# Local attention on patches of 8x4 instead of 8x8 pixels, in narrower tensor-engine tiles, and the two halves of a windowed sum issued together

## The chip, the cores and the metric

The kernel runs on one core of a Trainium2 chip, in one launch, in float32. The metric is device time in microseconds (us). Before the change the median of three runs is 1379.91 us (1377.02 to 1380.01).

The engines are called by the names of the profile: PE is the tensor engine (PEld its weight loads), DVE the vector engine, ACT the scalar engine, POOL the GpSimd engine, SP the engine that issues most DMAs. A "block" is eight image rows, 512 pixels, of one of four images.

## The reference

The input is x of 4 x 256 x 64 x 64. Layer 0 is an attention of each pixel over its 3x3 neighbours; layer 1 works on the 4096 tokens of an image: a gated sum over a window of 64 tokens, then a mixture of eight experts of which each token takes two.

```python
# layer 0: x = x + local attention of the group-normed x
q = (xc @ Wq + bq) * scale                      # every pixel
kf, vf = p @ Wk + bk, p @ Wv + bv               # padded image
logits = einsum('bhwc,bhwnc->bhwn', q, Kw)      # the 9 neighbours
ctx = einsum('bhwn,bhwnc->bhwc', softmax(logits), Vw)
out = ctx @ Wo + bo
...
# layer 1
g = sigmoid(tanh(x @ Wp.T + bp) @ Wg.T)
t = t + windowed_sum(g * x, 64) / windowed_sum(g, 64)   # x is the layer-normed t
t = t + sum over the top-2 experts of weight * (gelu(x @ w1[e] + b1[e]) @ w2[e] + b2[e])
```

## The kernel before, in words

There are 32 blocks (`NB`), 8 to an image. Weights are folded at the start (Wq with Wk, Wv with Wo), so that keys and values are the pixels themselves.

**Attention of a block** is in two generators. `produce(g)` projects the pixels to queries (`psq`, L509: four products of 512 columns) and writes them patch by patch. A patch is 8x8 pixels, its keys are the 10x10 pixels around, 100 in all (`NKEY`). A bias row is made by `psr` (L527, eight products whose outputs are 32 partitions high, so they lie in four column tiles of PE), taken up by ACT (`qrow`, L532) and turned by `psb` (L536). The logits `pss` (L547) are, for each of four groups of 128 pixels (`NG`), two patches by two channel halves: 16 products of 64 output rows and 100 columns. DVE adds the mask that keeps the 3x3 neighbours and takes the maximum (L554), ACT makes the exponentials (`pe`, L563) and their sums. `attend(g)` turns the weights with four transposes (`ptp`, L610), copies them on ACT (`pT`, L612), and mixes the pixels of the patch (`psc`, L621): 8 products over 100 keys, 64 output rows, 256 columns. ACT divides (`mix`, L627). Then come four-by-two transposes (`ptm`, L636), the output product (`pso`, L648) and the residual. The pixels by patch, `xp`, come from DRAM in a layout made beforehand (patch keys on partitions), loaded two blocks ahead (`load_xp`); `edges` overwrites the image's rim with the mean, on SP.

**Layer 1 of a block.** `tail(g)` transposes to tokens (`ptx`, L672), projects (`psp`, L685), makes the gate (`pj`, `z`: tanh and exp on ACT), copies the rows for the window (`wl`, L726 to L728) and sums over 64 tokens by two band matrices, `bandl` for the lower 64 outputs and `band` for the upper 64 (L736 and L737; 64 output rows each, so two column tiles). It does so three times a block: `psg` (36 columns) and `psw` twice (512 columns). Then it normalises, chooses the experts and makes the rows to be sent. `ranks(g)` counts (`psk`) and sends each token's row to its two experts' queues in DRAM with indirect DMAs on POOL (L870, eight a block).

**Experts.** `experts()` takes 135 slots of 256 rows: it fetches the rows (`sx`, SP), transposes them (`ptx`, L1023), copies on ACT (L1027), multiplies by w1 (`psh`, L1035), takes the gelu on ACT (`h`, L1041), multiplies by w2 (`psy`, L1054), adds the bias and weights on DVE (L1058, L1059), and adds the rows to the output with two indirect DMAs on POOL (L1072). A pair of these waits until the pair before has landed.

**Order.** All engines run their instructions in order. The main loop steps the generators `attend(g)`, `ranks(g-2)`, `tail(g-1)` and `produce(g+1)` in turn, and after each step lets the experts' stream go on as far as a table of due slots says (`follow`, 27 steps a block). The Tile framework then orders each engine's instructions by priority (place in this emission) and by its own estimate of when operands are ready. PSUM tiles come from `ps_a` (five buffers, all of the attention and tail) and `ps_s` (three, the experts).

```python
def window(to, part):
    nc.tensor.matmul(to[0:WIN], bandl, wl[part], start=True, stop=True)
    nc.tensor.matmul(to[WIN:P], band[:, WIN:P], wx[part], start=True, stop=True)
```

Of the kernel before, what the change touches and what calls it, by code (L numbers as in the profile page):

```python
# [46 lines left out]
FP = mybir.dt.float32  # L47
AF = mybir.ActivationFunctionType
# [4 lines left out]
P = 128  # L53
# [9 lines left out]
def hybrid_block_kernel(ctx: ExitStack, tc: tile.TileContext, ins: dict, out: bass.AP):  # L63
    nc = tc.nc
    x = ins["x"]
    B, C, FW, _ = x.shape
    W = FW - 2
    HW = W * W
    NC = C // P
    TB = 512  # L70
# [4 lines left out]
    WIN = 64  # L75
# [1 line left out]
    SCALE = float(C) ** -0.5  # L77
    EPS = 1e-5
    XBUFS = 4
    TH, TW = TB // W, 8  # L80
    KH, KW = TH + 2, TW + 2
    NKEY = KH * KW
    NP = W // TW
    QP = TH * TW
    NG = NP * QP // P
    PROWS = ins["xp"].shape[1]
    AHEAD = NBI + 2
    FETCH = 2
    I32, U32 = mybir.dt.int32, mybir.dt.uint32
# [20 lines left out]
    const = ctx.enter_context(tc.tile_pool(name="const", bufs=1))  # L110
    xsp = ctx.enter_context(tc.tile_pool(name="xsp", bufs=2))
    xp = ctx.enter_context(tc.tile_pool(name="xp", bufs=XBUFS))
    xtp = ctx.enter_context(tc.tile_pool(name="xtp", bufs=2))
    xpp = ctx.enter_context(tc.tile_pool(name="xpp", bufs=2))
    w1p = ctx.enter_context(tc.tile_pool(name="w1p", bufs=1))
    w2p = ctx.enter_context(tc.tile_pool(name="w2p", bufs=2))
# [5 lines left out]
    ps_a = ctx.enter_context(tc.tile_pool(name="ps_a", bufs=5, space=PSUM))  # L122
# [17 lines left out]
    def load_xp(g):  # L140
        if g >= NB:
            return
        t = xpp.tile([PROWS, NP, C], FP, tag="xp", name=f"xp_{g}")
        nc.sync.dma_start(t, ins["xp"][g])
        xpat[g] = t

# [70 lines left out]
    ident = const.tile([P, P], FP, tag="ident", name="ident")  # L217
# [26 lines left out]
    nc.vector.tensor_single_scalar(at_p[:, 1:2], at_p[:, 1:2], TW - 1, op=ALU.bitwise_and)  # L244
    nc.vector.tensor_copy(at_f, at_p)
    mask = const.tile([P, NKEY], FP, tag="mask", name="mask")
    near = w2p.tile([P, 2, KH, KW], FP, tag="pe", name="near")
    for d in range(2):
        nc.gpsimd.iota(
            near[:, d], pattern=[[1 - d, KH], [d, KW]], base=-1, channel_multiplier=0,  # L250
# [2 lines left out]
        part = near[:, d].rearrange("p a b -> p (a b)")  # L253
# [5 lines left out]
    )  # L259
    nc.vector.tensor_scalar(mask, mask, -NEG, NEG, ALU.mult, ALU.add)  # L260


    pick = const.tile([P, NG], FP, tag="pick", name="pick")
    nc.gpsimd.memset(pick, 0.0)
# [5 lines left out]
    band = const.tile([P, P], FP, tag="band", name="band")  # L270
# [9 lines left out]
    bandl = const.tile([P, WIN], FP, tag="bandl", name="bandl")  # L280
# [105 lines left out]
    for c in range(NC):  # L386
        cols = slice(c * P, (c + 1) * P)
        both = range(NC)
        ps = product(qk, [(wqT[:, o, cols], wkT[:, o, :]) for o in both], C, f"qk{c}")
# [79 lines left out]
    def edges(g):  # L469

        b, i = divmod(g, NBI)
        if g >= NB:
            return
        t, row = xpat[g], mean_row[b][0]
        rim, mean = xt[g], norm[b][0]
        nc.gpsimd.tensor_copy(
            rim[:, :, :, 0 : W + 2 : W + 1],
            mean.unsqueeze(2).unsqueeze(3).to_broadcast([P, NC, KH, 2]),
        )
        for at in ([0] if i == 0 else []) + ([KH - 1] if i == NBI - 1 else []):  # L480
            nc.gpsimd.tensor_copy(
                rim[:, :, at, :], mean.unsqueeze(2).to_broadcast([P, NC, W + 2])
            )
        lo = 1 if i == 0 else 0
        hi = KH - 1 if i == NBI - 1 else KH
        for at, h in ((0, 0), (KW - 1, NP - 1)):
            nc.sync.dma_start(
                t[lo * KW + at : (hi - 1) * KW + at + 1 : KW, h, :],
                row.partition_broadcast(hi - lo),
            )  # L490
        for kh in ([0] if lo else []) + ([KH - 1] if hi < KH else []):
            nc.sync.dma_start(
                t[kh * KW : (kh + 1) * KW],
                row.partition_broadcast(KW).unsqueeze(1).to_broadcast([KW, NP, C]),
            )

    def produce(g):
        if g >= NB:
            return
        b, i = divmod(g, NBI)  # L500
        _, rc, _ = norm[b]
        qks, qbb, ubs, kb = ask[b]
        t = xt[g]

        q = w2p.tile([P, NC, TB], FP, tag="q", name=f"q_{g}")
        for co in range(NC):
            ps = ps_a.tile([P, TB], FP, tag="a", name=f"psq_{g}_{co}")
            for ci in range(NC):
                nc.tensor.matmul(  # L509
                    ps.rearrange("p (r w) -> p r w", w=W),  # L510
                    qks[:, ci, co * P : (co + 1) * P], t[:, ci, 1 : TH + 1, 1 : W + 1],
                    start=(ci == 0), stop=(ci == NC - 1),
                )
            nc.scalar.activation(  # L514
                q[:, co].rearrange("p (h r c) -> p r h c", r=TH, c=TW),
                ps.rearrange("p (r h c) -> p r h c", r=TH, c=TW),
                AF.Identity, bias=qbb[:, co : co + 1], scale=rc[:, co : co + 1],
            )
            yield


        ps = ps_a.tile([P, P], FP, tag="a", name=f"psr_{g}")
        for ci in range(NC):
            for n in range(NG):
                to = ps[32 * n : 32 * (n + 1)].rearrange("p (j r c) -> p r j c", r=TH, c=TW)
                keys = t[:, ci, 1 : TH + 1, 1 + n * W // NG : 1 + (n + 1) * W // NG]
                nc.tensor.matmul(  # L527
                    to, ubs[:, ci, :], keys.rearrange("p r (j c) -> p r j c", c=TW),
                    start=(ci == 0), stop=(ci == NC - 1),
                )  # L530
        rows = w2p.tile([P, P], FP, tag="qrow", name=f"qrow_{g}")
        nc.scalar.activation(rows, ps, AF.Identity, bias=kb)  # L532
        yield
        qdotb = w2p.tile([P, NG], FP, tag="qdotb", name=f"qdotb_{g}")
        ps = ps_a.tile([P, NG], FP, tag="a", name=f"psb_{g}")
        nc.tensor.matmul(ps, rows, pick, start=True, stop=True)  # L536
        nc.vector.tensor_copy(qdotb, ps)
        yield

        top = w4p.tile([P, NG], FP, tag="stop", name=f"stop_{g}")  # L540
        s = w2p.tile([P, NG, NKEY], FP, tag="s", name=f"s_{g}")
        ps = ps_a.tile([P, NG, NKEY], FP, tag="a", name=f"pss_{g}")
        for n in range(NG):
            for ci in range(NC):
                for j in range(P // QP):
                    h = n * P // QP + j
                    nc.tensor.matmul(  # L547
                        ps[j * QP : (j + 1) * QP, n].rearrange("p (a b) -> p a b", b=KW),
                        q[:, ci, h * QP : (h + 1) * QP], t[:, ci, :, h * TW : h * TW + KW],
                        start=(ci == 0), stop=(ci == NC - 1),  # L550
                    )
        yield
        for n in range(NG):
            nc.vector.tensor_tensor_reduce(  # L554
                out=s[:, n], in0=ps[:, n], in1=mask, scale=1.0, scalar=NEG,
                op0=ALU.add, op1=ALU.max, accum_out=top[:, n : n + 1],
            )
        nc.vector.tensor_add(top, top, qdotb)
        nc.vector.tensor_sub(top, qdotb, top)
        pe = w2p.tile([P, NG, NKEY], FP, tag="pe", name=f"pe_{g}")  # L560
        den = w4p.tile([P, NG], FP, tag="den", name=f"den_{g}")
        for n in range(NG):
            nc.scalar.activation(  # L563
                pe[:, n], s[:, n], AF.Exp, bias=top[:, n : n + 1],
                accum_out=den[:, n : n + 1],
            )
        nc.vector.reciprocal(den, den)
        soft[g] = pe, den
        yield
# [16 lines left out]
    latest = []  # L586
# [12 lines left out]
    def attend(g):  # L599
        if g >= NB:  # L600
            return
        b, i = divmod(g, NBI)
# [2 lines left out]
        _, rc, back = norm[b]  # L605


        pt = ps_a.tile([P, NG, P], FP, tag="a", name=f"ptp_{g}")
        for n in range(NG):
            nc.tensor.transpose(pt[0:NKEY, n, :], pe[:, n, :], ident)  # L610
        pT = w2p.tile([P, NG, P], FP, tag="pT", name=f"pT_{g}")
        latest.append(nc.scalar.copy(pT[0:NKEY], pt[0:NKEY]).ins)  # L612
        yield

        mix = w1p.tile([P, NG, C], FP, tag="mix", name=f"mix_{g}")
        for pair in range(0, NG, 2):
            ps = ps_a.tile([P, 2, C], FP, tag="a", name=f"psc_{g}_{pair}")
            for n in range(2):
                for j in range(P // QP):
                    h = (pair + n) * P // QP + j  # L620
                    nc.tensor.matmul(  # L621
                        ps[j * QP : (j + 1) * QP, n, :],
                        pT[0:NKEY, pair + n, j * QP : (j + 1) * QP], xp_[0:NKEY, h, :],
                        start=True, stop=True,
                    )
            for n in range(2):
                nc.scalar.mul(mix[:, pair + n, :], ps[:, n, :], den[:, pair + n : pair + n + 1])  # L627
        load_xp(g + 2)
        edges(g + 2)
        yield  # L630
# [30 lines left out]
    def tail(g):  # L661
# [71 lines left out]
        rden = w2p.tile([P, NT], FP, tag="rden", name=f"rden_{g}")  # L733

        def window(to, part):
            nc.tensor.matmul(to[0:WIN], bandl, wl[part], start=True, stop=True)  # L736
            nc.tensor.matmul(to[WIN:P], band[:, WIN:P], wx[part], start=True, stop=True)  # L737

        ps = ps_a.tile([P, NT, 1 + E], FP, tag="a", name=f"psg_{g}")
        window(ps, (slice(None), slice(None), slice(C, C + 1 + E)))  # L740
# [478 lines left out]
```

## Time and profile before

| | |
|---|---|
| median of three runs | 1379.91 us |
| the profiled execution, its own time | 1383.41 us |
| its span | 1381.7 us |
| mean granted PE clock | 0.959 |
| PE passes (matmuls as the profile counts them) | 7148 |
| ACT table loads | 106, 1283 ns each |
| moved by DMA | 205.45 MB, 149 GB/s |
| patch loads `xp` | 32 of 896 KB |

A product in float32 shows as two passes in the profile. A busy time of PE holds a modelled tail after each pass, so the distance from one run's start to the next is the better price. In the page, a row of tenths has 40 slices of 34.5 us. In the timeline a row is a run of like instructions: start, length, engine, line, what is written from what, rows*columns of the weights, and how many passes.

### The profile page before, as it was taken

The numbers are of one execution on the slowest core, as the hardware profiler recorded it, in microseconds if no ns is written. First come the engines' busy times: TensorE is split into PE (matmuls) and PEld (weight loads), VectorE is DVE, ScalarE is ACT, GpSimd is POOL, SyncE is SP. The second block draws the span as 40 slices with busy tenths as digits, with TensorE's granted clock in tenths as the row PEclk, the third lists the DMA queues.
The fourth block names the chain that finished last, engine by engine and source line by source line (L and its number), as shares of the span: only waits on it lengthen the run. The fifth ranks groups of instructions, "written<-read, shape, count | busy, mean of one in ns | idle before, by whom it ended". The sixth has DMA issues, their size and how long they took to land. (4 is left out here: it accounts for less than half of the span.)

```text
span 1381.7 us, 24884 instructions
## 1 busy us (share of the span) xinstructions
PE 1215.3 (88%) x7148; PEld 845.7 (61%) x7148; DVE 882.3 (64%) x4298; ACT 824.5 (60%) x1619; POOL 736.7 (53%) x645
## 2 busy tenths in 40 slices
PE   5877879899999999999999999999999998957670
PEld 4543446566666766666666666666676666646560
DVE  4376767777776757676877677677756777722230
ACT  1445556677677667767677677767766675523320
POOL 2013223656565655566665656565665666754444
PEclk9998889999999999999999999999999999989995
DMA  9774555566766666676766566656676446665443
GB/s 306 190 237 136 134 161 154 153 162 151 166 165 165 172 149 166 168 166 160 164 156 149 132 171 137 150 124 163 147 156 134 100 98 140 151 144 83 85 65 38
DMA packets 138054, 205.45 MB, mean 149 GB/s; under 512 B 15697, under 2 KB 108609, under 8 KB 134209
## 3 DMA queue, kind: packets, MB, share of 16 engines
q1 hardware_dynamic: 84256, 131.48, 32.8%
q0 software_dynamic: 51168, 71.07, 28.6%
q10 hardware_dynamic: 2496, 1.32, 0.3%
q8 instruction: 59, 0.97, 0.3%
q14 instruction: 75, 0.61, 0.2%
HBM read 113.23 MB, written 90.59 MB: 148 GB/s over the span
## 5 line engine op out<-in xcount | busy, mean ns | idle before, releaser
L1072 POOL DMA_INDIRECT out<-sx x270 | 428.4, 1587 | 394.8 <-DVE sx L1059 69.6
L1054 PE MATMUL psy<-w,h 128*128 x1080 | 295.2, 397 | 31.0 <-DVE sx L1058 28.5
L870 POOL DMA_INDIRECT rows_in<-tok,rows x256 | 254.8, 995 | 105.5 <-issue 72.7
L1054 PEld LDWEIGHTS psy<-w,h 128*128 128x128 f32 x1080 | 193.8, 192 | 137.5 <-DVE sx L1058 70.8
L1035 PE MATMUL psh<-xc,w1s 128*128 128x256 f32 x1080 | 271.0, 393 | 1.3 <-ACT h L1041 1.1
L1035 PEld LDWEIGHTS psh<-xc,w1s 128*128 128x128 f32 x1080 | 201.4, 195 | 56.7 <-issue 23.1
L1058 DVE TENSOR_TENSOR sx<-psy,b2b 128x256 f32<-128x256 f32 x270 | 113.7, 421 | 161.7 <-PE psy L1054 137.1
L1041 ACT ACTIVATE h<-psh,w1s 128x256 f32<-128x256 f32 x270 | 112.9, 468 | 95.6 <-PE psh L1035 81.5
L1027 ACT COPY xc<-ptx 128x512 f32<-128x512 f32 x135 | 78.8, 584 | 139.1 <-PE ptx L1023 126.6
L648 PE MATMUL pso<-mixT,vo 128*128 128x512 f32 x256 | 127.2, 605 | 3.7 <-ACT mixT L637 1.9
L1023 PE MATMUL ptx<-ident,sx 128*128 128x128 f32 x540 | 85.9, 280 | 47.9 <-DMA sx<-rows_in 46.4
L509 PE MATMUL psq<-x,qks 128*128 128x512 f32 x256 | 126.0, 615 | 0.6 <-PE ptx L672 0.6
L1023 PEld LDWEIGHTS ptx<-ident,sx 128*128 128x128 f32 x540 | 67.3, 147 | 74.6 <-issue 48.9
L1059 DVE TENSOR_SCALAR sx<-sx 128x256 f32<-128x256 f32 x270 | 97.1, 360 | 3.7 <-DVE kb L463 0.3
L514 ACT ACTIVATE q<-psq,qbb,irc 128x512 f32<-128x512 f32 x64 | 49.7, 777 | 67.5 <-PE psq L509 62.9
L1016 ACT COPY w1s<-w1b 128x514 f32 x135 | 83.4, 619 | 6.6 <-DVE given L929 2.1
L554 DVE CUSTOM_DVE_ANT_0 s<-pss,mask 128x100 f32<-128x100 f32 x128 | 25.8, 257 | 89.0 <-PE ptx L1023 33.8
L769 ACT ACTIVATE x<-x,scale 128x256 f32<-128x256 f32 x128 | 66.4, 589 | 16.6 <-DVE scale L765 12.7
L737 PE MATMUL psw<-wx,band 128*64 128x512 f32 x128 | 74.1, 675 | 0.0
L736 PE MATMUL psw<-wl,bandl 128*64 128x512 f32 x128 | 73.7, 672 | 0.0
L685 PE MATMUL psp<-wpr,x1c 128*128 128x136 f32 x512 | 72.5, 284 | 0.0
L685 PEld LDWEIGHTS psp<-wpr,x1c 128*128 128x128 f32 x512 | 66.5, 191 | 4.9 <-ACT mix L627 2.3
(218 smaller groups left out, 2076.6 us busy)
## 6 DMA issues: line engine op xcount, KB each, us to landing
sx<-rows_in SPq DMA_DIRECT2D x135, 272.0 KB
xp<-in_xp SPq DMA_DIRECT2D x32, 896.0 KB
x<-in_x SPq DMA_DIRECT2D x32, 660.0 KB
xs<-in_xs SPq DMA_DIRECT2D x32, 512.0 KB
out<-x SPq DMA_DIRECT2D x32, 512.0 KB
out<-sx POOLq DMA_INDIRECT x270
rows_in<-tok,rows POOLq DMA_INDIRECT x256
rows_in<-blank SPq DMA_DIRECT2D x9, 272.0 KB
```

The source lines that it names most:

```text
L509: nc.tensor.matmul(ps.rearrange("p (r w) -> p r w", w=W), qks[:, ci, co * P : (co + 1) * P], t[:, ci, 1 : TH + 1, 1 : W + 1], start=(ci == ...
L648: nc.tensor.matmul(ps, vo[:, ci, co * P : (co + 1) * P], mixT[:, ci, :], start=(ci == 0), stop=(ci == NC - 1),)
L685: nc.tensor.matmul(ps[:, u, :], xc[:, ci, t * P : (t + 1) * P], wpr[:, ci, :], start=(ci == 0), stop=(ci == NC - 1),)
L870: return nc.gpsimd.indirect_dma_start(out=rows_in[:, :], out_offset=bass.IndirectOffsetOnAxis(ap=rows[:, c, t : t + 1], axis=0), in_=tok[: ...
L1016: nc.scalar.copy(w1s, w1b[:, e, :])
L1023: nc.tensor.transpose(pt[:, c, t * P : (t + 1) * P], xs[:, t, c * P : (c + 1) * P], ident)
L1035: nc.tensor.matmul(ps[:, f, :], w1s[:, o : o + P], xc[:, ci, :], start=(ci == 0), stop=(ci == NC - 1),)
L1041: inst = nc.scalar.activation(h[:, f, :], ps[:, f, :], AF.Gelu, bias=w1s[:, F1 + f : F1 + f + 1])
L1054: nc.tensor.matmul(ps[:, t, :], h[:, f, t * P : (t + 1) * P], w2[:, e, f, :], start=(f == 0), stop=(f == NC - 1),)
L1058: nc.vector.tensor_add(ys[:, t, :], ps[:, t, :], b2b[:, e, :])
L1059: nc.vector.tensor_scalar_mul(ys[:, t, :], ys[:, t, :], xs[:, t, bass.ds(e + C, 1)])
L1072: inst = nc.gpsimd.indirect_dma_start(out=out, out_offset=bass.IndirectOffsetOnAxis(ap=xs[:, t, C + E : C + E + 1].bitcast(U32), axis=0), ...
```

## The change

- Patches are 8x4 pixels: 60 keys (6x10) for 32 pixels, 16 patches a block; a group of 128 pixels holds four.
- The logits become 32 products of 32 output rows and 60 columns, in four column tiles.
- The exponentials are written into two lasting tiles whose rows are padded with zeros from 60 to 64 keys, so that two groups are turned by one 128x128 transpose: two transposes in place of four, and the copy `pT` has 256 columns on 128 partitions in place of 512 on 100.
- The weights of even groups then lie on partitions 0 to 63 and those of odd groups on 64 to 127. The pixels by patch are laid out likewise (128 partitions, 8 patches deep; 1024 KB in place of 896). The mixes become 16 products over 60 keys, 32 output rows, 256 columns, in two row halves by four column tiles; the halves write two PSUM tiles, which are open at the same time.
- The bias row's products stand directly before the logits; its ACT step, `psb` and the copy of its result come after them, and the generator has one stop less (five in place of six).
- In the windowed sum the upper half's product is given priority 0 and is ordered behind the lower half's, so that nothing goes between.
- `edges` writes a rim row in two DMAs, one for each half of the partitions.

```diff
-    TH, TW = TB // W, 8
+    TH, TW = TB // W, 4
...
+    HALF = P // 2
...
-        t = xpp.tile([PROWS, NP, C], FP, tag="xp", name=f"xp_{g}")
+        t = xpp.tile([P, NP // 2, C], FP, tag="xp", name=f"xp_{g}")
...
+    pes = []
+    for n in range(2):
+        t = const.tile([P, NG, HALF], FP, tag=f"pe_{n}", name=f"pe_{n}")
+        nc.gpsimd.memset(t, 0.0)
+        pes.append(t)
...
         for kh in ([0] if lo else []) + ([KH - 1] if hi < KH else []):
-            nc.sync.dma_start(
-                t[kh * KW : (kh + 1) * KW],
-                row.partition_broadcast(KW).unsqueeze(1).to_broadcast([KW, NP, C]),
-            )
+            for half in range(2):
+                at = half * HALF + kh * KW
+                nc.sync.dma_start(
+                    t[at : at + KW],
+                    row.partition_broadcast(KW).unsqueeze(1).to_broadcast([KW, NP // 2, C]),
+                )
...
-        ps = ps_a.tile([P, P], FP, tag="a", name=f"psr_{g}")
+        pr = ps_a.tile([P, P], FP, tag="a", name=f"psr_{g}")
...
-        rows = w2p.tile([P, P], FP, tag="qrow", name=f"qrow_{g}")
-        nc.scalar.activation(rows, ps, AF.Identity, bias=kb)
-        yield
-        qdotb = w2p.tile([P, NG], FP, tag="qdotb", name=f"qdotb_{g}")
-        ps = ps_a.tile([P, NG], FP, tag="a", name=f"psb_{g}")
-        nc.tensor.matmul(ps, rows, pick, start=True, stop=True)
-        nc.vector.tensor_copy(qdotb, ps)
-        yield
...
         yield
+        rows = w2p.tile([P, P], FP, tag="qrow", name=f"qrow_{g}")
+        nc.scalar.activation(rows, pr, AF.Identity, bias=kb)
+        qdotb = w2p.tile([P, NG], FP, tag="qdotb", name=f"qdotb_{g}")
+        pb = ps_a.tile([P, NG], FP, tag="a", name=f"psb_{g}")
+        nc.tensor.matmul(pb, rows, pick, start=True, stop=True)
+        nc.vector.tensor_copy(qdotb, pb)
+        yield
...
-        pe = w2p.tile([P, NG, NKEY], FP, tag="pe", name=f"pe_{g}")
+        pe = pes[g % 2]
...
-        pt = ps_a.tile([P, NG, P], FP, tag="a", name=f"ptp_{g}")
-        for n in range(NG):
-            nc.tensor.transpose(pt[0:NKEY, n, :], pe[:, n, :], ident)
+        pt = ps_a.tile([P, NG // 2, P], FP, tag="a", name=f"ptp_{g}")
+        for pair in range(NG // 2):
+            nc.tensor.transpose(
+                pt[:, pair, :], pe[:, 2 * pair : 2 * pair + 2, :].rearrange("p n k -> p (n k)"), ident
+            )
...
+        ps = [
+            ps_a.tile([P, NG // 2, C], FP, tag="a", name=f"psc_{g}_{half}") for half in range(2)
+        ]
+        for pair in range(NG // 2):
+            for half in range(2):
+                rows = slice(half * HALF, half * HALF + NKEY)
                 for j in range(P // QP):
                     nc.tensor.matmul(
+                        ps[half][j * QP : (j + 1) * QP, pair, :],
+                        pT[rows, pair, j * QP : (j + 1) * QP],
+                        xp_[rows, pair * P // QP + j, :],
                         start=True, stop=True,
                     )
...
         def window(to, part):
-            nc.tensor.matmul(to[0:WIN], bandl, wl[part], start=True, stop=True)
-            nc.tensor.matmul(to[WIN:P], band[:, WIN:P], wx[part], start=True, stop=True)
+            one = nc.tensor.matmul(to[0:WIN], bandl, wl[part], start=True, stop=True)
+            at = tc.cur_priority
+            tc.cur_priority = 0
+            two = nc.tensor.matmul(to[WIN:P], band[:, WIN:P], wx[part], start=True, stop=True)
+            tc.cur_priority = at
+            tc.add_manual_dep(
+                two.ins, one.ins.name,
+                mybir.DependencyInfo(
+                    mybir.DependencyClass.NoSync, mybir.DependencyReason.SCHED_ONLY
+                ),
+                reason="column tiles side by side",
+            )
```

## The prediction

> **What bounds the kernel now.** I read the page first, then busy time by stretches, then the timeline of the tensor engine over two blocks, the waits and the chain that ended last. The page's busy shares and its slices:
>
> ```profile
> PE 1215.3 (88%) x7148; PEld 845.7 (61%) x7148; DVE 882.3 (64%) x4298; ACT 824.5 (60%) x1619; POOL 736.7 (53%) x645
> ...
> PE   5877879899999999999999999999999998957670
> ```
>
> The tensor engine (PE) is nearly full from slice 7 to slice 33 of 40 and loose at both ends. The busy time by stretches (columns: core, stretch, its length, then busy time and count of each engine, granted clock, DMA share, GB/s) says how full:
>
> ```profile
> 600.00:800.00 200.00, 196.28 (x1189) 136.01 (x1188) 144.89 (x712) 141.81 (x272) 119.78 (x102) 1.00 0.67 157
> ...
> 1200.00:1250.00 50.00, 35.81 (x163) 29.44 (x162) 12.54 (x32) 15.93 (x33) 28.61 (x21) 0.86 0.66 153
> ```
>
> From 600 to 800 us PE is busy 98%, at full clock; VectorE (DVE) and ScalarE (ACT) 72% and 71%. From the logits of block 7 (225 us) to those of block 28 (986 us) it is 36.2 us a block. After 1200 us PE has slack. There the chain that ended last holds (start, length, what):
>
> ```profile
> 1267.54 3.95 DMA out<-sx
> ...
> 1272.34 1.55 POOL out L1072
> ...
> 1274.20 3.86 DMA out<-sx
> ```
>
> One pair of scatter-adds waits for the pair before it: a step of 6.5 us (issue 0.7, POOL 1.55, landing 3.9), 28 steps, 182 us to the end. No matmul lies in that path most of the time. So the block phase (to about 1200 us) is priced by PE, the last 180 us are not touched.
>
> The timeline of PE (start, length with its tail, passes as xN) gives the prices; the distance to the next start is what a run costs:
>
> ```profile
> 621.77 1.05 PE L736 MATMUL psw<-wl,bandl 128*64 128x512 f32 x2
> 622.95 1.13 PE L1054 MATMUL psy<-w,h 128*128 x4
> 624.01 1.07 PE L737 MATMUL psw<-wx,band 128*64 128x512 f32 x2
> ...
> 629.35 1.04 PE L672 MATMUL ptx<-ident,x1c 128*128 128x128 f32 x8
> 630.22 1.03 PE L1054 MATMUL psy<-w,h 128*128 x4
> ...
> 631.52 1.89 PE L509 MATMUL psq<-x,qks 128*128 128x512 f32 x4
> 633.34 1.95 PE L621 MATMUL psc<-xp,pT 100*64 100x256 f32 x16
> 635.22 1.99 PE L1035 MATMUL psh<-xc,w1s 128*128 128x256 f32 x8
> 637.05 1.09 PE L685 MATMUL psp<-wpr,x1c 128*128 128x136 f32 x8
> ...
> 644.15 0.68 PE L527 MATMUL psr<-x,ubs 128*32 128x128 f32 x16
> 644.76 1.99 PE L1035 MATMUL psh<-xc,w1s 128*128 128x256 f32 x8
> ```
>
> Each product is two passes. Eight 128-column transposes take 0.87 us (629.35 to 630.22): 0.109 us each, so 0.85 ns a column, 0.216 us for 256 columns, 0.432 for 512. **Column tiles do run side by side:** the 16 mix passes (64 columns wide, in two tiles) take 1.88 us where one after the other they would take 3.46; the 16 passes of the 32-wide psr take 0.61 where 16 x 0.109 is 1.74. **Going into a tiled run and out of it costs 0.344 us:** psq takes 1.82 for 4 x 0.432 = 1.73, psc 1.88 for 8 x 0.216 = 1.73, the psh behind it 1.83 for 1.73: 0.09 + 0.15 + 0.10. The same sum around paired psw runs is 0.344 too, every time.
>
> **The change part by part (PE).** Blocks are 32.
>
> Mixes (L621): 8 products of two tiles become 16 of eight tiles (two row halves by four columns). Now 8 rounds x 0.216 = 1.73 us; with eight at once 4 x 0.216 = 0.86. Row halves side by side are shown by no row. From both sides: 0.86 saved if they overlap fully, about -0.1 if not at all (8 rounds of four tiles, with 7 ns a round as psr has over its 0.108). [...] I take 0.80: 25.6 us over 32 blocks.
>
> Logits (L547): 16 products of 100 columns in two tiles, 16 rounds of 0.087 (the starts in the trace) = 1.39 us; after: 32 products of 60 columns in four tiles, 16 rounds of 60 x 0.85 = 0.051 plus psr's 7 ns: 0.93. Saved 0.46, 14.7 us in all. [...] The trace has the nearer row: within a psr round four starts lie 6.5 ns apart, and the 16 one-column passes of pqb L456 start within 0.13 us, 9 ns apart. [...]
>
> Transposes (L610): four of 0.109 become two: 0.22 saved, 7.0 us. ACT's copy of their result goes from 512 to 256 columns (586 to about 370 ns by the 256-column rows), the exponentials and mask steps from 100 to 60 columns: about 0.35 us of ACT and 0.16 of DVE a block, hidden today.
>
> Windows: in the order of the two programs 20 of 96 sums, 19 of them 512 columns wide, have an expert's matmuls between their halves, as at 621.77 and 624.01 above; none has after. A split one costs 4 x 0.432, a joined one 2 x 0.432: 19 x 0.864 = 16.4 us.
>
> Runs: the program of before goes into tiled runs 173 times, that of after 109 (psr stands directly before pss and has the same four tiles, the window runs merge): 64 x 0.344 = 22.0 us.
>
> PE's work falls by 25.6 + 14.7 + 7.0 + 16.4 + 22.0 = 85.7 us; some 3.4 us of the 36.2 of a steady block.
>
> **What else moves.** The patch load grows from 896 to 1024 KB (4 MB on 205, issued two blocks ahead, DMA share 0.67): nothing. Edges write the same two columns; a row of the rim is now two DMAs on SP instead of one, 8 more in all, behind the patch load and ahead of the next loads: below 0.1 us each at issue (the chain's SP pieces are 0.03), nothing. The steady zero padding is two fills at the start, when PE waits for data. The qrow step now follows pss, so its psb waits for ACT behind pso, as before. The loss is on ACT: in the order after, 14 blocks have a gelu between the first exponential and the other three, and the table loads go from 106 to 134. 28 x 1.283 us (the load's mean) = 36 us more on ACT, in a steady block of this kind 2.6 us on 25.6, less 0.35: 27.8 of some 33 us, 84%. Behind these loads on ACT stands the gelu h; psy waits for h, and everything behind psy on PE for that. ACT waits for psh today (81.5 us in all), so part is hidden: I charge a third, 12 us (ends 0 and 36).
>
> **The sum.** The 23 steady blocks hold 71 of the 85.7 us (1.48 each = 34; 16.4; 60 runs = 21). Off go 12 for the tables, and 9 for new waits: PE waits 0.9 us a block today (36.2 less 33.2 for all passes of a block at 0.85 ns a column, and six runs of 0.344) and the other engines come to 80%; I take a doubling on ten of the blocks. That leaves 50. The six blocks before experts run (27 us each with PE some 75% busy) hold 10; half counts, 5. The last three lie where scatter-adds already follow at 6.5 to 7 us (from 1144 us on): 1 of 5. Together 56: the profiled execution took 1383.4 us (span 1381.7), so 1327; the median of the runs shown, 1379.9, is 3.5 lower: 1324.
>
> **The rivals.**
> - Nothing is lost to waits: 71 + 8 = 79 us, 1301. For it: DVE and ACT end below 85%. Against: in-order engines with no slack left.
> - Row halves do not overlap: the mixes save nothing, some 22 us less: 1346. Only a trace can tell.
> - ACT takes most of it: the 36 us of table loads fall on PE in full, and the adds, at four pairs a block (26 us at 6.5, POOL's eight give instructions of 1 us between), hold it at times: 24 + 12 less, 1360.
> - Slower: the exponential, first in line on ACT, waits for DVE's maximum (the waits have ACT pe on DVE stop at up to 5.9 us), and the gelu queued behind it keeps psy, and with it all of PE, standing. In the 14 blocks with split exponentials PE loses this and two table loads. It decides from 85.7/14 = 6.1 us a block on; at 5.9 + 2.6 = 8.5 the loss is 119, 33 more than PE saves: 1413. Against it: today that wait comes four times in all, early, where PE is idle anyway.
>
> **Chances.** As summed, 1305 to 1340: 0.55. Nothing lost: 0.14. No row overlap: 0.10. ACT takes most: 0.10. Within 0.3%, about what a measurement of this kernel can tell from none: 0.04, all of these losses at once. Slower: 0.07. Range 1292 to 1366. Faster 0.89, same 0.04, slower 0.07.
>
> **What would show it.** A psc run of 32 passes in about 1.0 us against 1.9; psr and pss together about 1.6 against 2.2; no psy between psw halves; PE's busy time down by 80; blocks of 33.5 us; the last 28 add steps at 6.5 us still. Wrong it would be if psc stays at 1.9 (row halves in turn), if pss comes near 1.9 (a floor per start), or if waits of psy on ACT h appear by tens of us.

## The result and the profile after

The changed kernel takes 1389.63 us (median of 20 runs, 1382.23 to 1397.74) against 1380.34 for the kernel before (20 runs): ratio 1.006, 95% interval 1.0039 to 1.0081. It is slower by 0.6%. The profiled execution takes 1394.86 us, its span 1392.9, its mean granted clock 0.942 where it was 0.959. I had said 1324.

The page of the kernel after: busy times, then two of its rows of tenths.

```profile
PE 1169.3 (84%) x8620; PEld 833.3 (60%) x8620; DVE 878.7 (63%) x4298; ACT 844.5 (61%) x1647; POOL 739.9 (53%) x647
...
PE   5978799799988989899988999999899888867770
...
PEclk9999889999999999999999999999999999889995
```

PE is busy for 46 us less, and yet the program is longer: PE's share has gone from 88% to 84%. The row of tenths has eights and sevens where the row of before had nines from slice 7 on. By the start of `psr` in each block, the changed kernel is 22 us ahead at block 7 (198 us against 220) and 11 us behind at block 31: the loss falls in the steady blocks. The stretch from 600 to 800 us (columns as in the prediction):

```profile
600.00:800.00 200.00, 181.19 (x1357) 129.35 (x1356) 138.74 (x689) 145.72 (x271) 119.96 (x102) 0.97 0.62 152
```

PE is busy 181.2 us of 200 where it was 196.3, at 0.97 of the clock where it was 1.00. No other engine has risen to be the bound (ACT 73%, DVE 69%). So what is lost is waiting, and part of it slower clock.

**What came as priced.** Timeline of PE, kernel after, one block:

```profile
664.18 0.62 PE L748 MATMUL psw<-wl,bandl 128*64 128x512 f32 x1
664.19 0.62 PE L751 MATMUL psw<-wx,band 128*64 128x512 f32 x1
664.64 0.59 PE L748 MATMUL psw<-wl,bandl 128*64 128x512 f32 x1
...
670.30 1.09 PE L632 MATMUL psc<-xp,pT 60*32 60x256 f32 x32
671.32 1.99 PE L1057 MATMUL psh<-xc,w1s 128*128 128x256 f32 x8
...
681.95 0.68 PE L536 MATMUL psr<-x,ubs 128*32 128x128 f32 x16
682.44 1.04 PE L547 MATMUL pss<-x,q 128*32 128x60 f32 x38
683.90 0.33 PE L547 MATMUL pss<-x,q 128*32 128x60 f32 x4 [0.43 <-issue]
684.65 0.32 PE L547 MATMUL pss<-x,q 128*32 128x60 f32 x5 [0.41 <-issue]
685.43 0.47 PE L547 MATMUL pss<-x,q 128*32 128x60 f32 x17 [0.47 <-issue]
685.83 3.23 PE L1057 MATMUL psh<-xc,w1s 128*128 128x256 f32 x8
```

The mixes `psc` take 1.02 us (670.30 to 671.32) against 1.88: the eight 64x32 tiles of a round start 6 to 7 ns apart and overlap (four rounds at 0.216 are 0.86). The two halves of a window sum start 5 to 13 ns apart in all 192 pairs of passes. Both were forecast. The logits were not: from 682.44 to 685.83 `pss` takes 3.39 us. It breaks off after 38 passes, and then comes in pieces of 4 and 5 passes, about 0.77 us apart. "issue" says that it waited for nothing that the profile shows. In other blocks the same 64 passes take 0.98 us.

**The larger loss** is a wait of `psy`. Timeline of all engines, kernel after:

```profile
713.01 0.28 DVE L356 TENSOR_SCALAR ve_a<-tmv_a 128x4 f32<-128x4 f32 x1
...
713.62 0.98 POOL L892 DMA_INDIRECT rows_in<-tok,rows  x1 [0.31 <-issue]
...
714.91 0.96 POOL L892 DMA_INDIRECT rows_in<-tok,rows  x1 [0.30 <-issue]
...
716.18 0.96 POOL L892 DMA_INDIRECT rows_in<-tok,rows  x1 [0.30 <-issue]
717.16 1.06 POOL L357 TENSOR_TENSOR trstd_a<-ve_a,nhalf 128x4 f32<-128x4 f32 x1
...
718.25 0.61 DVE L703 SCALAR_TENSOR_TENSOR pj<-psp,trstd_a,bp 128x128 f32<-128x128 f32 x2 [2.62 <-POOL trstd_a L357]
718.78 0.17 DVE L706 COPY y<-psp 128x16 f32<-128x16 f32 x1
718.86 0.41 DVE L1080 TENSOR_TENSOR sx<-psy,b2b 128x256 f32<-128x256 f32 x1
...
719.33 1.13 PE L1076 MATMUL psy<-w,h 128*128 x4 [2.71 <-DVE sx L1080]
...
720.29 1.65 PE L648 MATMUL ptm<-ident,mix 128*128 128x128 f32 x8
```

Read it from the bottom. PE stands 2.71 us, since `psy` needs the PSUM tile that DVE's `sx` empties. DVE stands 2.62 us ahead of `sx`, at `pj`, which needs the root of the first norm, `trstd_a`. The root is a 1.06 us instruction on POOL (`pow`). Its input was ready at 713.3, but in POOL's order it stands behind four sends, 1.28 us each; the first began at 712.3, so three of them make the wait. The queues of three engines stand in line, PE behind DVE behind POOL, and none of the three is full. And after the pause PE runs at half clock for 3.4 us: the eight `ptm` transposes show 1.65 us where others of that shape show 1.04.

In other blocks the experts' scatter-adds (`out`) stand ahead of the root too. Timeline of POOL, kernel after:

```profile
750.56 1.64 POOL L1094 DMA_INDIRECT out<-sx  x1 [0.31 <-issue]
752.51 1.00 POOL L892 DMA_INDIRECT rows_in<-tok,rows  x1 [0.30 <-issue]
753.81 0.97 POOL L892 DMA_INDIRECT rows_in<-tok,rows  x1 [0.30 <-issue]
754.81 1.05 POOL L357 TENSOR_TENSOR trstd_a<-ve_a,nhalf 128x4 f32<-128x4 f32 x1
```

The sums by waits, kernel after and then before:

```profile
DVE pj L703 <- POOL trstd_a L357: 68.8, 26, 6.7
PE psy L1076 <- DVE sx L1080: 66.0, 37, 8.7
...
PE pss L547 <- issue: 12.9, 30, 0.6
```

```profile
DVE pj L691 <- POOL trstd_a L350: 29.6, 21, 5.1
PE psy L1054 <- DVE sx L1058: 28.5, 34, 6.4
```

Now all pauses, from the single starts of PE's passes between 200 and 1000 us. A pause is what lies between two starts beyond the streaming of the first pass (0.85 ns a column; at half clock twice that, as 128-column transposes start 213 ns apart there and 109 at full clock), where it is over 0.45 us. Pauses sum to 20.3 us before and 90.1 after. Of the 90.1, 56.7 are ahead of `psy` (17.4 before), 34.3 of them in 14 pauses directly behind `psq` while DVE waits at `pj`; 17.2 lie inside `pss` (none before). Another 11.2 stand in seven blocks in which a gelu, between two table loads on ACT, splits the four exponentials: 3.7 ahead of `psh`, 4.1 between two `psy`, 3.4 ahead of `psg` (none before). Half clock is granted for 47.8 us in place of 11.2; outside the pauses it is 42.2 in place of 7.4, and the extra 34.8 us are worth some 17, by half of their length. So about 70 + 17 = 87 us of pauses and slow clock stand against the work saved.

One more fact of the order: in the blocks of that stretch DVE's idle time ahead of the first `pj` has a median of 0.79 us before and 2.3 after. Before, the first `pj` came behind `comb`, `comb` and `weight` in 10 of 22 blocks; after, it comes ahead of them in 16 of 21. The root, once its input is ready, waits 52.3 us in all before and 76.0 after. In these waits POOL is busy with sends for 38.4 us before and 46.1 after (four sends stand ahead in 5 of 21 blocks, mostly two in the others), and with scatter-adds for 3.3 and 15.0. So the scatter-adds have grown more than the sends.

The last stretch is as it was: the last 28 steps of adds are at some 6.5 us each.

### The profile page after: what moved, and what is told of

Read it like the earlier page. It is cut to its first block, busy times and chain, and to the rows that moved or that the text cites. A ratio compares the mean times of both kernels' runs of the same rounds, so it can differ in the third digit from the quotient of the medians.

```text
span 1392.9 us, 27845 instructions
## 1 busy us (share of the span) xinstructions
PE 1169.3 (84%) x8620; PEld 833.3 (60%) x8620; DVE 878.7 (63%) x4298; ACT 844.5 (61%) x1647; POOL 739.9 (53%) x647
## 5 line engine op out<-in xcount | busy, mean ns | idle before, releaser
L1076 PE MATMUL psy<-w,h 128*128 x1080 | 299.0, 400 | 70.6 <-DVE sx L1080 66.0
L1076 PEld LDWEIGHTS psy<-w,h 128*128 128x128 f32 x1080 | 199.4, 196 | 159.3 <-DVE sx L1080 104.0
L1045 PE MATMUL ptx<-ident,sx 128*128 128x128 f32 x540 | 89.1, 290 | 45.7 <-DMA sx<-rows_in 41.2
L1045 PEld LDWEIGHTS ptx<-ident,sx 128*128 128x128 f32 x540 | 70.1, 153 | 68.4 <-issue 49.8
L703 DVE SCALAR_TENSOR_TENSOR pj<-psp,trstd_a,bp 128x128 f32<-128x128 f32 x128 | 41.8, 346 | 76.0 <-POOL trstd_a L357 68.8
L649 ACT ACTIVATE mixT<-ptm,iback,irc 128x512 f32<-128x512 f32 x64 | 46.8, 771 | 50.2 <-PE ptm L648 49.7
```

Source lines behind the costliest of these rows:

```text
L1045: nc.tensor.transpose(pt[:, c, t * P : (t + 1) * P], xs[:, t, c * P : (c + 1) * P], ident)
L1076: nc.tensor.matmul(ps[:, t, :], h[:, f, t * P : (t + 1) * P], w2[:, e, f, :], start=(f == 0), stop=(f == NC - 1),)
```

## The experiments

**Theories.** A (root): what costs the time is the queue sends, root, `pj`, `sx`, `psy`. B (windows): joined windows (the two halves of a window sum issued together) gain nothing, since `psy` loses its place between the halves. C (logits): the stretched `pss` comes of its 128 PE instructions in a row, or of its narrow tiles. e1, e2, e3 and e6 ran on one chip, e4, e5, e7 and e8 on another one; on both the kernel before takes 1383 to 1387 us.

**e1, the root on DVE.** The file has a second root, `rsqrt_v`, eleven small DVE instructions, used for the second norm.

```diff
-        norm1[g] = token_norm([x1T[:, t, :] for t in range(NT)], f"a{g}")
+        norm1[g] = token_norm([x1T[:, t, :] for t in range(NT)], f"a{g}", rsqrt_v)
```

> The changed kernel with one edit: the reciprocal root of the first token norm is made on DVE (the routine that the second norm uses already) and not on POOL. Root theory: of the kernel after, psy waits 57 us between 200 and 1000 us because DVE's pj stands ahead of the expert's add and waits for POOL's root, which stands behind four sends. Then DVE's idle time before pj goes from 76 to under 20 us, the waits of psy over 0.45 us from 57 to about 20 us, the half-clock time in that stretch from 48 to about 20 us, and the median to 1345 (1335 to 1360). The stalls inside the logits (17 us) stay. Rival, instruction supply or ACT's table loads being the cause: the time stays within 0.5% of the kernel after (1383 to 1396), the waits of psy only move to another line.

1341.74 us, ratio 0.9676 (0.9619 to 0.9733). Waits of the kernel with the root on DVE:

```profile
PE psy L1076 <- DVE sx L1080: 22.2, 25, 4.5
```

The 66.0 us have become 22.2, though DVE has 46 us more to do; pauses of PE fall from 90 to 60 us, half clock from 47.8 to 17.1, and no pause is left ahead of `psy` with DVE at `pj`. The stretched `pss` stays (16.6 us). The edit moves ACT's order as well: it has 120 table loads in place of 134, 18 us less work.

**e2, the same edit in the kernel before.**

> The kernel before with the same edit as e1. Root theory: before, pj waits for the root too (29.6 us of DVE's time) but PE rarely waits behind it (20 us of gaps in all between 200 and 1000 us), so the time stays within 0.5% of before (1373 to 1387). If the root were a general brake the time would fall by some 30 us here too, and the gain of e1 would not belong to the change.

1394.6 us, ratio 1.0065 (1.0038 to 1.0093). So e1's gain isn't a general merit of that root: before the change it costs 0.65%. With the root on DVE in both, the change is worth 1394.6 - 1341.7 = 53 us on that chip.

**e3, the joined windows alone,** in the kernel before.

> The kernel before with the joined windows alone. By the prices of the prediction: 19 split sums joined (16.4 us) and 23 runs fewer (8 us), 24 us less PE work, no new table loads, no denser instructions: 1358 to 1366. Rival, that PE's time freed in this order always comes back as waits: the time stays within 0.5% (1373 to 1387) and PE's idle time grows by 20 us or more.

1389.01 us, ratio 1.0008 (0.9982 to 1.0033): a miss. PE's busy time falls by 16 us of the 24 that were forecast, and the pauses rise from 20 to 49 us: 15.8 behind `ptx` with DVE busy throughout, 11.2 behind `psq` at `pj`. That a joined window brings `psy` to DVE's queue earlier would explain it; it was not tested by itself.

**e4, the change without the joined windows.**

> The changed kernel with the window sums issued as before the change: patches, tiles, transposes and the new place of the bias row alone. If the waits on POOL's root come from the joined windows (which in e3 alone made 11 us of them), psy waits little behind pj here (under 10 us between 200 and 1000 us) and the time lies at 1350 to 1370. Rival: the shorter mixes make them, since psy comes to its wait earlier in the block whatever the windows do: 20 us or more of psy's waits behind pj, and 1385 to 1400.

1397.31 us, ratio 1.0108 (1.0077 to 1.0139). The pauses behind `psq` at `pj` are there still, 32.8 us in 11. So the new patches bring them by themselves, not the windows.

**e7, joined windows and root on DVE, old patches.**

> The kernel before with the joined windows (e3) and the first norm's root on DVE (e2). Each alone brought nothing (ratios 1.0008 and 1.0065). If the root stands in the way of any PE time that is freed, the two together give the windows' 24 us less the 6 of the longer DVE work: ratio 0.985 to 0.992. Rival: DVE, 46 us busier, is what PE waits for here (15.8 us of e3's waits had DVE busy throughout): ratio 1.000 to 1.010, and the gain of e1 needs the patches.

1384.24 us, ratio 1.0008 (0.9987 to 1.003). Against the kernel before that is nothing, but against e2, which has the same root, the joined windows are worth 0.6%, some 8 us of the 24 priced. No pause falls at the root any more; those behind `ptx` with DVE busy throughout stay (16.3 us).

**e6, the row products apart again.** `qrow`, `psb` and a stop go back ahead of the logits, as in the kernel before:

```diff
         pr = ps_a.tile([P, P], FP, tag="a", name=f"psr_{g}")
         ...
+        rows = w2p.tile([P, P], FP, tag="qrow", name=f"qrow_{g}")
+        nc.scalar.activation(rows, pr, AF.Identity, bias=kb)
+        yield
+        ...
+        nc.vector.tensor_copy(qdotb, pb)
+        yield
         ...
```

> The changed kernel with the bias row, its ACT step and psb put back to where they were before the change; patches, tiles, mixes and windows stay. In this order an expert's psh (16 instructions in 1.8 us) comes directly before the logits and not psp and psr (64 instructions in 1.5 us), and the table loads fall from 134 to 106. Supply theory, that the logits stall when PE's instructions have come fast before them: the logits' runs take 1.0 us in nearly every block (now 2 to 3.5 us in 13), the gaps inside fall from 17 to under 3 us, at the price of 32 more runs (11 us): 1360 to 1375. Rival, that 32-wide tiles of 60 columns stall by themselves: the stalls stay at 2 to 3.5 us in a dozen blocks, the time at 1390 to 1400. Root theory: psy's waits stay near 57 us.

1415.85 us, ratio 1.0217 (1.0161 to 1.0273): the theory of that expectation, that instructions come too fast ahead of the logits, fell. Nor do fewer table loads make the kernel fast: it has 106 of them, as the kernel before. `pss` is stretched in nearly every block, 27.8 us of pauses in place of 17. Timeline of PE in that kernel:

```profile
703.76 1.21 PE L556 MATMUL pss<-x,q 128*32 128x60 f32 x49
705.41 0.32 PE L556 MATMUL pss<-x,q 128*32 128x60 f32 x5 [0.45 <-issue]
706.15 0.33 PE L556 MATMUL pss<-x,q 128*32 128x60 f32 x6 [0.42 <-issue]
706.91 0.33 PE L556 MATMUL pss<-x,q 128*32 128x60 f32 x4 [0.43 <-issue]
```

The pieces of 4 to 6 passes start 0.74 to 0.76 us apart. From such pauses I then estimated a supply of some 11 instructions (5 passes and their weight loads) per 0.65 us, 59 ns each, which a run of 128 would outrun: the sequencer theory of the next expectations. No view shows such a supply.

**e5, more instructions in the kernel before:** its logits in 32 products of 50 columns, so 128 instructions in place of 64 in two tiles, not four.

```diff
+            for u in range(2):
+                part = slice(u * KH // 2, (u + 1) * KH // 2)
...
-                        ps[j * QP : (j + 1) * QP, n].rearrange("p (a b) -> p a b", b=KW),
-                        q[:, ci, h * QP : (h + 1) * QP], t[:, ci, :, h * TW : h * TW + KW],
...
+                            ps[j * QP : (j + 1) * QP, n].rearrange("p (a b) -> p a b", b=KW)[:, part],
+                            q[:, ci, h * QP : (h + 1) * QP],
+                            t[:, ci, part, h * TW : h * TW + KW],
...
```

> The kernel before with each product of the logits cut in two of 50 columns, everything else as before: 32 products of 64 rows, so as many PE instructions a block (128) as after the change, still in two column tiles. Sequencer theory: a run of 128 instructions outruns what PE's sequencer hands over (in the stalls of e6 some 11 instructions in 0.65 us); the runs take 3 to 3.7 us with gaps of 0.65 us, as those of e6 do, and the kernel is slower by 32 x 1.8 us, ratio 1.03 to 1.05. Rival, narrow tiles: 32-wide tiles or their PSUM writes make the stalls; then the runs take 32 rounds of 0.059 (the round of psg, with 64-wide weights), 1.9 us without gaps over 0.2, ratio 1.005 to 1.012.

1424.17 us, ratio 1.0307 (1.0268 to 1.0346). Most of its `pss` runs take 3.2 to 3.8 us: after some 54 of the 64 passes the starts break off, and every 5 or 6 passes there lie 0.53 to 0.65 us between two of them. Timeline of PE in that kernel:

```profile
708.18 1.91 PE L549 MATMUL pss<-x,q 128*64 128x50 f32 x53
710.45 0.38 PE L549 MATMUL pss<-x,q 128*64 128x50 f32 x6 [0.35 <-issue]
711.18 0.37 PE L549 MATMUL pss<-x,q 128*64 128x50 f32 x5 [0.35 <-issue]
```

So neither narrow tiles nor the new layout is needed: on this chip 128 instructions in a row are enough.

**e8, e1 with the logits in two halves** (64 instructions, a stop, 64 instructions: `if n == NG // 2: yield`).

> e1 with one more stop: the logits are issued in two halves of 16 products, and other matmuls of at least 2 us stand between them; the table loads fall from 120 to 104 by the new order. Sequencer theory: halves of 64 instructions are covered by what is queued (as the 64 of the kernel before are), no stall over 0.2 us; 16.6 us of stalls go between 200 and 1000 us, some 22 in all, 32 more runs at 0.344 cost 11: 1325 to 1338. Rival: the stalls move into the halves, and the time is 1345 to 1360.

1352.05 us, ratio 0.9779 (0.9737 to 0.982): a miss. The pauses in `pss` fall from 16.6 to 5.8 us, but the waits of `psy` rise from 31.2 to 37.4 and half clock from 17.1 to 20.5. It is not ahead of e1.

**e9 and e10, with the root on DVE: the whole change again, and without joined windows,** on one chip. It happened to be another one, on which the kernel before takes 1348.5 us.

> The full change with the root of the first norm on VectorE a second time, beside the version without joined windows on the same chip. If the first result holds, 1338 to 1346 us, ratio 0.964 to 0.972; if it was particular to one chip, nearer 0.98.

> The change without its joined windows, and with the root of the first norm on VectorE. Theory: the windows are worth their PE time (16 us fewer) where PE stays busy, so this kernel stands 8 to 16 us behind the full change with the root on VectorE: 1350 to 1358 us, ratio 0.975 to 0.983. Rival: joined windows give back what they save as waits of the expert's second product, as they did in the kernel before (ratio 1.0008 alone): the same time as the full change with the root on VectorE within 4 us, ratio 0.966 to 0.972.

e9: 1295.35 us, ratio 0.9614 (0.9575 to 0.9654). e10: 1311.45 us, ratio 0.9712 (0.9682 to 0.9742). The joined windows are worth 16.1 us here, twice what they are worth with the old patches (e7 against e2). By the prices of the prediction it would be 20: 19 split sums (16.4 us), and 11 tiled runs fewer at 0.344. And not one `pss` run from 200 us on takes over 1.3 us, neither in e9 nor in e10. e1 and e9 are the same program: from block 9 to block 30 e1 needs 31 us more, and 21 of them lie between passes of `pss`. Timeline of PE in e9:

```profile
660.89 0.68 PE L536 MATMUL psr<-x,ubs 128*32 128x128 f32 x16
661.39 1.05 PE L547 MATMUL pss<-x,q 128*32 128x60 f32 x64
```

**e11 and e12, the changed kernel and e5 again.** These ask whether the stretching goes with the chip or with the program. The chip was a further one, on which the kernel before takes 1350.13 us.

> The changed kernel as it is, once more, on whatever chip it falls. In the last pair of runs, on a chip where the kernel before takes 1348 us and not 1383, no logits run was stretched (0.98 to 1.2 us), though the programs were like those stretched to 2 to 3.5 us before. If the stretching belongs to the chip, then where the kernel before takes about 1350 us the logits runs are clean here too, and the ratio is 0.98 to 0.995, the waits for POOL's root being all that is left of the loss; where it takes about 1380 us, stretched runs in 10 to 15 blocks and a ratio of 1.004 to 1.010. If the stretching belongs to the program (the root on POOL), stretched runs on either chip.

> The kernel before with its logits cut into 128 instructions in place of 64, once more, beside the changed kernel on the same chip. If the supply of instructions belongs to the chip: logits runs of 3.2 to 3.8 us and a ratio near 1.03 where the kernel before takes about 1380 us; runs near 1.4 to 2.0 us and a ratio of 0.995 to 1.01 where it takes about 1350. If it belongs to the program alone: 3.2 to 3.8 us on either.

e11: 1359.37 us, ratio 1.0082 (1.0051 to 1.0112). e12: 1360.43 us, ratio 1.0078 (1.0052 to 1.0104). Timeline of PE and waits of e11, then the timeline of e12:

```profile
697.11 0.68 PE L536 MATMUL psr<-x,ubs 128*32 128x128 f32 x16
697.60 1.06 PE L547 MATMUL pss<-x,q 128*32 128x60 f32 x64
```

```profile
DVE pj L703 <- POOL trstd_a L357: 77.6, 26, 9.7
PE psy L1076 <- DVE sx L1080: 57.4, 39, 6.0
```

```profile
634.30 2.07 PE L549 MATMUL pss<-x,q 128*64 128x50 f32 x64
670.46 2.07 PE L549 MATMUL pss<-x,q 128*64 128x50 f32 x64
```

The stretching is gone on this chip for the same two programs (from 260 us on `pss` takes 0.98 to 1.18 us in e11, after two runs of 1.5 and 1.75 us; e5's 3.2 to 3.8 us are 2.0, with two of 2.2 and 2.3): it goes with the chip, or with the chip's state at that hour, and not with the program. But the ratio of the changed kernel is as bad as before, and the wait for POOL's root is as large. I had expected 0.98 to 0.995 on such a chip, so I still gave the stretched logits too much of the loss. e11 against e9, both on quick chips, gives what moving the root is worth: spans 1356.1 and 1291.8, 64 us apart. Between 200 and 1000 us, pauses differ by 72.0 - 28.3 = 44 us, and half clock outside the pauses by 33.2 - 6.8 = 26 us, worth 13: together 57.

Not all of that is the root. Of the 72.0 us of pauses in e11, some 48 fall while DVE stands at `pj`, and 11 stand at exponentials split by a gelu; e9 has neither. So most of the 64 us is the queue ahead of the root, and a smaller part is ACT's order, which moved with the edit.

| ratio to the kernel before | root on POOL | root on DVE |
|---|---|---|
| old patches | 1 | 1.0065 (e2) |
| old patches, joined windows | 1.0008 (e3) | 1.0008 (e7) |
| new patches | 1.0108 (e4) | 0.9712 (e10) |
| new patches, joined windows (the change) | 1.006; 1.0082 (e11) | 0.9676 (e1); 0.9614 (e9) |

e1 beats both kernels, on two chips.

## Why the prediction was wrong, by its own steps

- **PE's work.** Mixes saved 0.86 us a block for 0.80 charged (`psc` takes 1.02 us), transposes 0.16 (0.44 to 0.27) for 0.22; no window sum is split, and tiled runs went from 173 to 109, as said. Right, though e10 against e9 gives 16.1 us for the joined windows where these prices give 20. The 0.80 was an estimate between the ends 0.86 and -0.1, nearer the first since psr's rounds of four tiles take 0.117 us for 0.108: no run shows that term itself, and what `psc` shows is 0.86, full overlap.
- **New waits: 9 us. This is the step that failed.** I doubled today's slack of 0.9 us on ten blocks, on the ground that "the other engines come to 80%". A share says nothing of an order. The pauses of PE grew by 70 us in 800. Of these, 17 lie in `pss` and 11 at split exponentials, which belong to the next two terms; the other 42 stand against these 9, and half clock took some 17 more, a cost that the sum did not have at all. Most of the 42 is `psy` held by `pj` at POOL's root (34 us, none before), and with the root off POOL these pauses are gone (e1, e9). The line that held the answer was in the profile before: `pj` waits 29.6 us for `trstd_a`, in 21 places. It cost PE nothing then: between 200 and 1000 us no pause of PE fell behind `psq` with DVE at `pj`.
- **Logits: 0.46 us saved a block.** Where clean, `pss` takes 0.98 us for 0.93 forecast (in e9 its starts lie 13 ns apart on the mean). But on the slower chips the run breaks off and goes on in pieces of 2 to 5 passes, some 0.75 us apart: in the changed kernel 12 blocks take 1.9 to 3.6 us, 25 us too many, against 14.7 forecast as gain. I had asked only how close to each other starts can lie, and judged that by the short runs in the trace (in the kernel before psr's 16 passes start within 0.40 us, psc's 16 take 1.88 in every block). A run of 128 was not among them. That a supply of instructions runs dry fits the pauses, but was not shown. As to the sign of the result it hardly mattered: e11 has no stretched run after 260 us and is 0.8% slower.
- **Table loads: 12 us.** ACT's loads did go from 106 to 134, and the charge was about right: the pauses of PE at split exponentials are 11.2 us between 200 and 1000 us. The path is longer than I had it. The first wait is for the gelu, ahead of `psh`; then DVE waits for the last exponential at `den`, with `sx` and so `psy` behind it; then `wl` is late on ACT for `psg`. In the waits of the kernel after:

```profile
DVE den L574 <- ACT pe L570: 28.0, 17, 2.7
```

- **The sum.** With the root on DVE in both kernels the change is worth 53 us (e2 to e1) where I had 56. That this is so near is luck. By the starts of `psr`, 21 us are gained up to block 6, where I had 5, and 24 from there to block 29, where I had 50; the stretched logits of e1, some 25 us, are about what is missing there. Why the first blocks gained so much was not followed up.
- **The rivals.** Row overlap was full, ACT did not take it, and the rival that ended slower named the wrong wait: not the exponential on DVE's maximum with `gelu` behind it, but `pj` on POOL's root with `sx` behind it. Its shape (an engine stands at an early instruction, the expert's product waits behind it, all of PE with that; at 715 us DVE for 2.62 us and PE for 2.71) was the right one; that is all it had right. That the 87 us of pauses and slow clock lie near its point of decision, 85.7, is chance: the one is a count in 800 us, the other a sum over all blocks.
- **What would show it.** psc at 1.02, and no `psy` between window halves: as said. PE's busy time fell by 46, not 80; passes at half clock count longer (the eight `ptm` transposes 1.65 us for 1.04), and in e9, which has little of it, it is 1130.0, 85 below the kernel before. Blocks 11 to 25 take 38.3 us each (574 us for 15) where 33.5 was said; the same blocks took 36.8 before.

**Open:** why `pss` breaks off on two chips and not on the two others. The instruction DMAs are alike (71 packets of 16 KB in e1 and in e9), and few pauses inside `pss` overlap one (22 of 152 in the changed kernel, e1, e5 and e6). What put the scatter-adds ahead of the root, and how much of DVE's longer wait comes of `pj` standing ahead of `comb`, was not separated; nor was why joined windows pay more with the new patches (DVE, which `psy` meets in e3 and e7, is as busy in e9 as in e7).

## What to carry to other kernels

When the fullest engine is made faster, list every instruction of the next engine that waits for a third one, however short the sum of it, and ask what stands behind it in its queue: here 1 us of `pow`, behind POOL's sends of 1.28 us and its scatter-adds. Moving it off that queue gave 64 us (e11 against e9), more than the 53 us that the change is worth without it (e2 to e1). A wait that is covered today is a debt that falls due with the cover (29.6 us of `pj` at the root before, 68.8 after). And before an edit is called worthless, test it again once a wait that hides its gain is gone: the joined windows brought nothing in the kernel before (e3), some 8 us with the root on DVE (e7 against e2), and 16 us with the new patches besides (e9 against e10). The new patches, at 1.0108 with the root on POOL (e4), are at 0.9712/1.0065 = 0.965 with it on DVE (e10 over e2, each against the kernel before on its own chip).

## What the runs showed of the hardware

- Eight tiles of 64x32 (two row halves by four columns) run at once in float32: 32 passes of 256 columns in 1.02 us, the eight of a round started 6 to 7 ns apart.
- Between 200 and 1000 us of the changed kernel, all 8 pauses of PE over 2.8 us come with half clock for 3.4 or 6.8 us, which begins within the pause or up to 1.3 us behind it. At half clock 128-column transposes start 213 ns apart, at full clock 109. By half of the half-clock time behind the pause, an estimate, it adds a fifth to nine tenths of the pause. In e11 6 of 8 such pauses do, and those of 3.0 and 3.5 us do not; in e9 one of 2.6 us does.
- Chips of one kind differ by 2.5% on one program (1348 and 1350 us against 1383 and 1387 us), each seen at one time only. On a slower one a logits run of 128 PE instructions mostly takes 3.2 to 3.8 us where a quicker one needs 2.0 (e5, e12). Instruction times are alike on both (the 512-column pass starts 431 ns after the one before it, the 128-column one 109).
- A round of logits, by the starts of its passes, takes 53 ns for 60 columns in four tiles (e9; 0.85 ns a column is 51) and 59 ns for 50 columns in two tiles (e12; 43 by that price). With 100 columns in two tiles it is 87, so cutting these in two made them longer, 118 for 87.
